# Cross-attention with layer norm: transposes of the identity ahead of x, x evacuated by two engines, and another order of loads, statistics and queries up to slot 2

## The chip, the cores and the metric

The kernel runs on one core of a Trainium2 chip. The metric is the device time of one execution in microseconds (us).

## The reference

Everything is float32. x has 8 batches of 256 rows of 1024; the context has the same shape and serves as keys and as values; there are 32 heads of 32.

```python
xn = (x - mean) * rsqrt(var + 1e-5) * gamma + beta
Q, K, V = split_heads(xn @ Wq.T), split_heads(ctx), split_heads(ctx)
scores = einsum('bhsd,bhtd->bhst', Q, K) * 32 ** -0.5    # masked
attn = einsum('bhst,bhtd->bhsd', softmax(scores), V)      # heads merged again
return x + attn @ Wout.T
```

## The kernel before

**Work and slots.** A unit of work n is one batch and one group of four heads, so there are 64 units, eight to a batch. Slot n of the main loop does the scores of unit n+1, the values of unit n-2, the projection of the batch before, one or two queries that later slots need, and the softmax of unit n+1. The schedule is manual: each engine does its instructions in the order in which the program issues them, and semaphores join the engines. A DMA is issued on SyncE's queue, in program order too.

**A softmax** (`softmax_parts`) takes four tiles, one for each head, each in a PSUM bank of its own (pool `ps_s`, four banks). VectorE adds the mask and finds the row minimum (L391), ScalarE takes the exponential with its sum (L395), VectorE inverts the sum (L402), GpSimd multiplies (L404, `normalize`), VectorE transposes 32x32 blocks (L410, `blocks`), ScalarE copies a part aside (L416), and four DMAs finish the transposition. `new_q` are queries that ScalarE copies out of PSUM after the exponentials; `fill` is a list of other pieces of work that `fill_in` puts between these steps; `between` are loads issued between the four DMAs.

**Queries.** `make_q` (L316) projects eight chunks of normalized x with eight of Wq into one PSUM bank, `copy_q` (L324, L326, L330) takes it to SBUF. The second query of a slot uses the bank of the projection and follows the softmax in program order. `BATCH0` says how many queries each of the first eight slots makes; after that each slot makes one. An fp32 matmul shows as two instructions in the profile, a transpose as one.

**The lead-in.** Only the first batch takes x through TensorE with gamma and beta in the evacuation. `ln_stats` (L205 to L211) takes the statistics of one half of the rows (s = 0 or 1), its last step a power on GpSimd; `ln_norm` (L224 on VectorE) normalizes. `transpose_x0(s)` puts eight 128x128 transposes into two PSUM banks, four in each (L238). `copy_x0` evacuates one of the eight, on ScalarE (L247) or VectorE (L249), with gamma and beta. `first_q(s)` multiplies them with the first part of Wq (L258) and ScalarE copies one half of query 0 (L262). Batch 1 is transposed in slots 0 and 1 (`transpose_x1`, L275, and `copy_x1`, L279 and L281), without gamma: `fold` (L339) multiplies Wq by gamma on GpSimd, one part in each slot. Later batches are transposed by VectorE and DMAs. GpSimd also makes sums of Wout (`sum_wo`, L172) and of the attention output (L522) for a projection with seven products instead of eight (L532; its third product is S2).

Of the kernel before, what the change touches and what calls it, by code (L numbers as in the profile page):

```python
# [46 lines left out]
F32 = mybir.dt.float32  # L47
# [12 lines left out]
def xattn_kernel(  # L60
# [52 lines left out]
    ctx.enter_context(tc.manual_schedule())  # L113


    xs, ks, vs, rs = {}, {}, {}, {}

    def load_x(b, s, h=None):

        if b not in xs:  # L120
            xs[b] = xp.tile([P, NS, D], F32, tag="x", name=f"x_{b}")
        cols = ds(0, D) if h is None else ts(h, 512)
        nc.sync.dma_start(xs[b][:, s, cols], x[b, ts(s, P), cols])
# [31 lines left out]
    def load_wq(o):  # L155
        nc.sync.dma_start(wq[:, o], wq_[o])
# [20 lines left out]
        for h in range(2):  # L177
            load_x(0, s, h)
    load_wq(0)
    for s in range(NS):  # L180
        load_x(1, s)
    load_wq(1)
    load_k(0)
    nc.sync.dma_start(mk, mask.to_broadcast([P, B, T]))
    for o in range(2, 5):
        load_wq(o)
    load_k(2)
    load_v(0)
    load_wq(5)


    xnTs, qs, mvs, rstds = {}, {}, {}, {}
# [3 lines left out]
    def ln_stats(b, s, parts=range(3)):  # L196

        if s == 0 and 0 in parts:
            mvs[b] = sm.tile([P, NS, 2], F32, tag="mv", name=f"mv_{b}", bufs=2)
            rstds[b] = sm.tile([P, NS], F32, tag="rstd", name=f"rstd_{b}", bufs=2)  # L200
        if 0 in parts:
            sts[b, s] = sm.tile([P, 2, 6], F32, tag="st", name=f"st_{b}_{s}", bufs=2)
        for h in range(2):
            if h in parts:
                nc.vector.bn_stats(sts[b, s][:, h, :], xs[b][:, s, ts(h, 512)])  # L205
        if 2 not in parts:
            return
        nc.vector.bn_aggr(mvs[b][:, s, :], sts[b, s].rearrange("p h k -> p (h k)"))
        ve = sm.tile([P, 1], F32, tag="ve", name=f"ve_{b}_{s}", bufs=2)
        nc.vector.tensor_scalar(ve, mvs[b][:, s, 1:2], LN_EPS, None, ALU.add)  # L210
        nc.gpsimd.tensor_tensor(rstds[b][:, s : s + 1], ve, mhalf[:, :1], ALU.pow)  # L211

    def ln_norm(b, s, engine):
        if engine is nc.scalar:
            shift = sm.tile([P, 1], F32, tag="shift", name=f"shift_{b}_{s}", bufs=2)
            nc.gpsimd.tensor_scalar(
                shift, mvs[b][:, s, 0:1], rstds[b][:, s : s + 1], -1.0, ALU.mult, ALU.mult
            )
            engine.activation(
                xs[b][:, s, :], xs[b][:, s, :], AF.Identity,  # L220
                bias=shift, scale=rstds[b][:, s : s + 1],
            )
            return
        engine.tensor_scalar(  # L224
            xs[b][:, s, :], xs[b][:, s, :], mvs[b][:, s, 0:1], rstds[b][:, s : s + 1],
            ALU.subtract, ALU.mult,
        )
# [5 lines left out]
    def transpose_x0(s):  # L233

        for g in range(2):
            px0[s, g] = ps_v.tile([P, NC // 2, P], F32, tag="pv", name=f"px0_{s}_{g}")
            for i in range(NC // 2):
                nc.tensor.transpose(  # L238
                    px0[s, g][:, i, :], xs[0][:, s, ts(NC // 2 * g + i, P)], ident
                )  # L240
# [7 lines left out]
        else:  # L248
            nc.vector.tensor_scalar(to, pt, g, b, ALU.mult, ALU.add)  # L249

    def first_q(s):

        if s == 0:
            pqs[0] = ps_q.tile([P, 512], F32, tag="pq", name="pq_0")
            qs[0] = qp.tile([P, S + 1], F32, tag="q", name="q_0")
        cols = ds(0, P) if s == 0 else ds(P, P + 1)
        for c in range(NC):
            nc.tensor.matmul(  # L258
                pqs[0][:, cols], wq[:, 0, c, :], xnT0[:, c, cols],
                start=(c == 0), stop=(c == NC - 1),  # L260
            )
        nc.scalar.activation(qs[0][:, cols], pqs[0][:, cols], AF.Copy, scale=NEG_SCALE)  # L262

# [82 lines left out]
    def mask_bias(b):  # L346

        mbs[b] = sm.tile([P, T], F32, tag="mb", name=f"mb_{b}", bufs=2)
        nc.vector.tensor_scalar(mbs[b], mk[:, b, :], 1.0, -MASKED, ALU.subtract, ALU.mult)
# [11 lines left out]
                    start=True, stop=True,  # L361
                )

    def softmax(*args):
        for _ in softmax_parts(*args):
            pass

    def softmax_parts(n, new_q=(), between=(), hooks={}, fill=()):

        fill = list(fill)

        def fill_in():
            if fill:
                fill.pop(0)()

        pss = scs[n]
        pT = pTs[n] = ptp.tile([P, 2, NI, NH, NS, K], F32, tag="pT", name=f"pT_{n}")  # L380
        pc = asp.tile([P, NI, NH, NS, K], F32, tag="pc", name=f"pc_{n}")
        es, mns, dens = {}, {}, {}

        def exps(j, part=range(NS)):
            if 0 in part:
                es[j] = ep.tile([P, NS, T], F32, tag="e", name=f"e_{n}_{j}")
                mns[j] = sm.tile([P, NS], F32, tag="mn", name=f"mn_{n}_{j}")
                dens[j] = sm.tile([P, NS], F32, tag="den", name=f"den_{n}_{j}")
            e, mn, den = es[j], mns[j], dens[j]
            for s in part:  # L390
                nc.vector.tensor_tensor_reduce(  # L391
                    out=e[:, s, :], in0=pss[j][:, s, :], in1=mbs[n // NQ], scale=1.0,
                    scalar=NO_SCORE, op0=ALU.add, op1=ALU.min, accum_out=mn[:, s : s + 1],
                )
                nc.scalar.activation(  # L395
                    e[:, s, :], e[:, s, :], AF.Exp, bias=mn[:, s : s + 1], scale=-1.0,
                    accum_out=den[:, s : s + 1],
                )

        def normalize(j):  # L400
            rden = sm.tile([P, NS], F32, tag="rden", name=f"rden_{n}_{j}")
            nc.vector.reciprocal(rden, dens[j])  # L402
            for s in range(NS):
                nc.gpsimd.tensor_scalar(  # L404
                    es[j][:, s, :], es[j][:, s, :], rden[:, s : s + 1], 1.0,
                    ALU.mult, ALU.mult,
                )

        def blocks(j):
            nc.vector.transpose(  # L410
                pT[:, :, :, j, :, :].rearrange("p a i s k -> p (a i) s k"),
                es[j].rearrange("p s (b t) -> p b s t", t=K),
            )

        def aside(j):
            nc.scalar.copy(pc[:, :, ts(j, 2)], pT[:, 1, :, ts(j, 2)])  # L416

        if n == 0:
            for j in range(NH):
                exps(j, (0,))  # L420
            yield
            exps(0, (1,))
            exps(1, (1,))
            exps(2, (1,))
        else:
            exps(0)
            for done in list(pvs):
                copy_at(done)
            exps(1)
            exps(2)  # L430
        normalize(0)
        exps(3, (1,) if n == 0 else range(NS))
        if n <= NQ:
            for q in new_q:
                copy_q(q)
        for hook in hooks.get(0, ()):
            hook()
        normalize(1)
        fill_in()
        blocks(0)  # L440
        for hook in hooks.get(1, ()):
            hook()
        normalize(2)
        fill_in()
        blocks(1)
        aside(0)
        normalize(3)
        fill_in()
        blocks(2)
        fill_in()  # L450
        blocks(3)
        while fill:
            fill_in()
        if n > NQ:
            for q in new_q:
                copy_q(q)
        aside(1)

        for r in range(2):
            nc.sync.dma_start(pT[ts(2 * r, K), 1], pT[ts(2 * r + 1, K), 0])  # L460
        for load in between:
            load()
        for r in range(2):
            nc.sync.dma_start(pT[ts(2 * r + 1, K), 0], pc[ts(2 * r, K)])
        yield

    def values(n):
        pvs[n] = [
# [102 lines left out]


    START = 2
    BATCH0 = (1, 2, 1, 2, 1, 2, 1, 2)
    new_qs, made = [], START
    for n in range(N):
        k = min(BATCH0[n] if n < NQ else 1, N - made)
# [43 lines left out]
    ln_stats(0, 1, (0,))  # L621
    ln_norm(0, 0, nc.vector)
    ln_stats(0, 1, (1, 2))
    nc.gpsimd.tensor_copy(xnT0[:, :, S], bet)
    ln_norm(0, 1, nc.vector)
    ln_stats(1, 0, (0, 1))
    transpose_x0(0)
    for c in range(NC):
        copy_x0(0, c, nc.scalar)
    first_q(0)  # L630
    transpose_x0(1)
    scores(0, (0,))
    for c in range(NC):
        copy_x0(1, c, nc.vector if c % 2 else nc.scalar)
    mask_bias(0)
    first = softmax_parts(
        0, (1,), [partial(load_wq, 6), partial(load_wq, 7)], {},
        [partial(ln_norm, 1, 0, nc.vector), partial(ln_norm, 1, 1, nc.vector)],
    )
    next(first)  # L640
    first_q(1)
    make_q(1, second=True, chunks=range(2))
    scores(0, (1,))
    make_q(1, second=True, chunks=range(2, NC))
    ln_stats(1, 1)
    ln_stats(1, 0, (2,))
    for _ in first:
        pass


    last = None
# [157 lines left out]
```

## Time and profile before

| what | value |
|---|---|
| median of 3 runs | 599.85 us (599.37 to 600.08) |
| profiled execution, its own time | 600.28 us |
| span of the profiled execution | 598.5 us |
| TensorE busy | 579.2 us (97%) |
| VectorE busy | 462.4 us (77%) |
| ScalarE busy | 404.4 us (68%) |
| GpSimd busy | 346.7 us (58%) |
| TensorE busy in 0 to 100 us | 87.87 us |
| TensorE busy in 100 to 500 us | 399.99 us |

PE is TensorE's matmuls, PEld its weight loads, DVE VectorE, ACT ScalarE, POOL GpSimd, SP SyncE; a q after the name is the engine's queue. An L with a number is the line of the kernel. Groups read "line engine operation output<-inputs": px is x transposed in PSUM, xnT the normalized x transposed, pq a query in PSUM, q the query in SBUF, sc the scores, e the exponentials, pT the probabilities transposed. Matmuls are pipelined, so that a busy TensorE need not be one at its peak.

### The profile page before, as it was taken

What the parts mean: (1) busy time and instruction counts of PE and PEld (TensorE: products, weight loads), DVE (VectorE), ACT (ScalarE), POOL (GpSimd) and SP (SyncE); (2) the same over time, 40 slices, a digit from 0 to 9 for tenths busy, and PEclk for the clock granted to TensorE, in tenths of its full rate; (3) what the DMA queues carried; (4) which work ended last, traced back from release to release, by engine and by line L of the source; (5) the groups of instructions that cost most, each with busy time, mean ns of one, the idle gap of its engine ahead of it and who ended that gap; (6) DMA issues with size and microseconds to landing.
All of it is one profiled execution on the core that took longest, in us unless ns stands there. A gap on an engine that the chain in (4) does not pass through costs nothing.

```text
span 598.5 us, 18847 instructions
## 1 busy us (share of the span) xinstructions
PE 579.2 (97%) x6648; PEld 386.7 (65%) x6648; DVE 462.4 (77%) x1677; ACT 404.4 (68%) x1378; POOL 346.7 (58%) x628
## 2 busy tenths in 40 slices
PE   5789999999999999999999999999999999998897
PEld 4578877666766666766666667666676666654443
DVE  4879888788887978788787887878786677779901
ACT  3677788677767767776766876777676576667700
POOL 1468898889448444666438553584545554386600
PEclk9989999999999999999999999999999999999999
DMA  8477678545764557634774556644555364465541
GB/s 310 150 217 222 191 224 245 172 126 155 211 182 143 154 150 222 194 84 155 202 204 144 141 154 171 208 133 132 178 155 168 108 174 141 114 188 176 161 126 70
DMA packets 42063, 101.13 MB, mean 169 GB/s; under 512 B 8560, under 2 KB 8560, under 8 KB 41968
## 3 DMA queue, kind: packets, MB, share of 16 engines
q1 hardware_dynamic: 41680, 99.91, 56.8%
q8 instruction: 53, 0.87, 0.6%
q14 instruction: 42, 0.34, 0.2%
q10 hardware_dynamic: 288, 0.01, 0.0%
HBM read 51.65 MB, written 8.39 MB: 100 GB/s over the span
## 4 chain that ended last, share of the span: by engine, by line
PE 84%; POOL 5%; DVE 5%; ACT 2%; issue 2%; DMA 1%; SPq 0%; POOLq 0%; DVEq 0%
PE pq L316 33%; PE po_S L532 18%; PE pv L475 10%; PE sc L359 10%; PE po_A L532 8%; POOL e L404 5%; PE po L560 3%; DVE e L391 2%; ACT e L395 1%; DVE pT L410 1%; DMA x<-in_x_dram 1%; PE pq L258 1%; PE po_last L560 0%; PE px L238 0%; POOL wq L339 0%
## 5 line engine op out<-in xcount | busy, mean ns | idle before, releaser
L404 POOL TENSOR_SCALAR e<-e,rden 128x256 f32<-128x256 f32 x512 | 237.1, 480 | 175.1 <-DVE rden L402 172.1
L395 ACT ACTIVATE e<-e,mn 128x256 f32<-128x256 f32 x512 | 253.8, 501 | 54.6 <-DVE mn L391 53.4
L316 PE MATMUL pq<-xnT,wq 128*128 128x256 f32 (+1 forms) x1008 | 232.4, 384 | 0.2 <-ACT q L326 0.2
L410 DVE STREAM_TRANSPOSE pT<-e 128x512 f32<-128x512 f32 x256 | 181.3, 709 | 53.8 <-POOL e L404 44.7
L316 PEld LDWEIGHTS pq<-xnT,wq 128*128 128x128 f32 x1008 | 190.1, 191 | 44.3 <-issue 18.0
L391 DVE CUSTOM_DVE_ANT_0 e<-sc,mb 128x256 f32<-128x256 f32 x512 | 185.1, 417 | 32.0 <-PE sc L359 31.3
L416 ACT COPY pc<-pT 128x512 f32<-128x512 f32 x128 | 79.1, 618 | 86.9 <-DVE pT L410 54.7
L532 PE MATMUL po_S<-wo,at 128*128 128x512 f32 x224 | 106.9, 603 | 2.0 <-DVE u L544 1.3
L395 ACT ACTIVATION_READ_ACCUMULATOR e<-e,mn 128x1 f32 x512 | 98.0, 191 | 0.0
L359 PEld LDWEIGHTS sc<-k,q 32*128 32x128 f32 x1024 | 46.4, 184 | 51.0 <-issue 20.9
L359 PE MATMUL sc<-k,q 32*128 32x256 f32 x1024 | 74.1, 401 | 4.9 <-ACT q L324 3.2
L475 PE MATMUL pv<-pT,v 64*32 64x128 f32 x4096 | 74.3, 274 | 0.9 <-ACT at L487 0.9
L475 PEld LDWEIGHTS pv<-pT,v 64*32 64x32 f32 x4096 | 57.1, 105 | 23.5 <-issue 14.4
L532 PEld LDWEIGHTS po_S<-wo,at 128*128 128x128 f32 x224 | 40.7, 189 | 37.1 <-issue 31.8
L532 PE MATMUL po_A<-wo,at 128*128 128x512 f32 x112 | 51.9, 598 | 0.0
L402 DVE RECIPROCAL rden<-den 128x2 f32<-128x2 f32 x256 | 39.3, 154 | 7.5 <-ACT e L395 5.1
L391 DVE DVE_READ_ACCUMULATOR2_ANT mn<- 128x1 f32 x512 | 42.6, 83 | 0.0
L532 PEld LDWEIGHTS po_A<-wo,at 128*128 128x128 f32 x112 | 20.8, 190 | 19.1 <-issue 17.9
L211 POOL TENSOR_TENSOR rstd<-ve,mhalf 128x1 f32<-128x1 f32 x16 | 8.8, 549 | 41.3 <-DVE ve L210 41.3
L487 ACT COPY at<-pv 128x128 f32<-128x128 f32 x128 | 26.0, 251 | 8.2 <-PE pv L475 8.2
L330 ACT ACTIVATE q<-pq,qb 128x256 f32<-128x256 f32 x48 | 22.5, 470 | 9.5 <-PE pq L316 9.5
L532 PE MATMUL po_S<-wo,s 128*128 128x512 f32 x56 | 26.9, 606 | 0.6 <-DVE r L552 0.6
(51 smaller groups left out, 293.8 us busy)
## 6 DMA issues: line engine op xcount, KB each, us to landing
v<-in_kv_dram SPq DMA_DIRECT2D x32, 512.0 KB, 4.6
pT<-pT SPq DMA_DIRECT2D x128, 128.0 KB, 2.3
pT<-pc SPq DMA_DIRECT2D x128, 128.0 KB, 4.1
k<-in_kv_dram SPq DMA_DIRECT2D x32, 256.0 KB, 3.3
x<-in_x_dram SPq DMA_DIRECT2D x14, 512.0 KB, 5.0
r<-in_x_dram SPq DMA_DIRECT2D x28, 256.0 KB, 4.5
out_dram<-r SPq DMA_DIRECT2D x28, 256.0 KB, 3.0
xnT<-xe SPq DMA_DIRECT2D x96, 64.0 KB, 3.3
```

What stands on the lines that cost most here:

```text
L316: nc.tensor.matmul(pqs[n], wq[:, o, c, :], xnTs[b](c), start=(c == 0), stop=(c == NC - 1),)
L330: nc.scalar.activation(q[:, :S].rearrange("p (s a k) -> p a s k", s=NS, a=NA), pqs.pop(n).rearrange("p (a s k) -> p a s k", s=NS, a=NA), A ...
L359: nc.tensor.matmul(scs[n][j][:, s, :], qs[n][r, ts(s, P)], ks[n - n % 2][r, n % 2, :], start=True, stop=True,)
L391: nc.vector.tensor_tensor_reduce(out=e[:, s, :], in0=pss[j][:, s, :], in1=mbs[n // NQ], scale=1.0, scalar=NO_SCORE, op0=ALU.add, op1=ALU.m ...
L395: nc.scalar.activation(e[:, s, :], e[:, s, :], AF.Exp, bias=mn[:, s : s + 1], scale=-1.0, accum_out=den[:, s : s + 1],)
L402: nc.vector.reciprocal(rden, dens[j])
L404: nc.gpsimd.tensor_scalar(es[j][:, s, :], es[j][:, s, :], rden[:, s : s + 1], 1.0, ALU.mult, ALU.mult,)
L410: nc.vector.transpose(pT[:, :, :, j, :, :].rearrange("p a i s k -> p (a i) s k"), es[j].rearrange("p s (b t) -> p b s t", t=K),)
L416: nc.scalar.copy(pc[:, :, ts(j, 2)], pT[:, 1, :, ts(j, 2)])
L475: nc.tensor.matmul(pvs[n][r][j * HD : (j + 1) * HD], vs[n - n % 2][ts(r, 2 * K), i, ds(n % 2 * P + j * HD, HD)], pT[ts(r, 2 * K), :, i, j, ...
L487: nc.scalar.copy(ats[b][:, c, :, ts(r, 2), :], pv.rearrange("p a s k -> p s a k"))
L532: nc.tensor.matmul(pos[b], operand(b, name)[:, c], wo[:, which, c], start=begins and c == 0, stop=c == NK - 1, skip_group_check=not begins,)
```

## The change

Before x arrives, TensorE makes 32 transposes of the identity into a PSUM tile that nothing reads. Eight tiles of the first half of x are evacuated by both engines (six by ScalarE, two by VectorE), those of the second half by bank: the first bank by ScalarE, the second by VectorE. k of the first units and the mask are loaded ahead of x of batch 1, and the last two parts of Wq at the start and not in the first softmax. The first softmax is no longer cut in two: its exponentials follow the copy of both halves of query 0, and the statistics of x of batch 1 become pieces between its steps. Slots 0 to 7 make 2, 2, 1, 1, 2, 1, 2, 1 queries and no longer 1, 2, 1, 2, 1, 2, 1, 2.

```diff
--- before.py
+++ after.py
@@ -113,6 +113,11 @@
     ctx.enter_context(tc.manual_schedule())
 
 
+    busy = ps_s.tile([P, P], F32, tag="sc", name="busy")
+    for _ in range(32):
+        nc.tensor.transpose(busy, ident, ident)
+
+
     xs, ks, vs, rs = {}, {}, {}, {}
 
     def load_x(b, s, h=None):
@@ -177,16 +182,17 @@
         for h in range(2):
             load_x(0, s, h)
     load_wq(0)
-    for s in range(NS):
-        load_x(1, s)
-    load_wq(1)
     load_k(0)
     nc.sync.dma_start(mk, mask.to_broadcast([P, B, T]))
+    load_x(1, 0)
+    load_wq(1)
+    load_x(1, 1)
     for o in range(2, 5):
         load_wq(o)
     load_k(2)
     load_v(0)
-    load_wq(5)
+    for o in range(5, 8):
+        load_wq(o)
 
 
     xnTs, qs, mvs, rstds = {}, {}, {}, {}
@@ -248,16 +254,16 @@
         else:
             nc.vector.tensor_scalar(to, pt, g, b, ALU.mult, ALU.add)
 
-    def first_q(s):
+    def first_q(s, chunks=range(NC)):
 
         if s == 0:
             pqs[0] = ps_q.tile([P, 512], F32, tag="pq", name="pq_0")
             qs[0] = qp.tile([P, S + 1], F32, tag="q", name="q_0")
         cols = ds(0, P) if s == 0 else ds(P, P + 1)
-        for c in range(NC):
+        for c in chunks:
             nc.tensor.matmul(
                 pqs[0][:, cols], wq[:, 0, c, :], xnT0[:, c, cols],
-                start=(c == 0), stop=(c == NC - 1),
+                start=(c == chunks[0]), stop=(c == chunks[-1]),
             )
         nc.scalar.activation(qs[0][:, cols], pqs[0][:, cols], AF.Copy, scale=NEG_SCALE)
 
@@ -361,11 +367,7 @@
                     start=True, stop=True,
                 )
 
-    def softmax(*args):
-        for _ in softmax_parts(*args):
-            pass
-
-    def softmax_parts(n, new_q=(), between=(), hooks={}, fill=()):
+    def softmax(n, new_q=(), between=(), hooks={}, fill=()):
 
 
 
@@ -416,20 +418,20 @@
             nc.scalar.copy(pc[:, :, ts(j, 2)], pT[:, 1, :, ts(j, 2)])
 
         if n == 0:
-            for j in range(NH):
-                exps(j, (0,))
-            yield
-            exps(0, (1,))
-            exps(1, (1,))
-            exps(2, (1,))
+            for s in range(NS):
+                for j in range(NH):
+                    exps(j, (s,))
+            fill_in()
+            normalize(0)
+            fill_in()
         else:
             exps(0)
             for done in list(pvs):
                 copy_at(done)
             exps(1)
             exps(2)
-        normalize(0)
-        exps(3, (1,) if n == 0 else range(NS))
+            normalize(0)
+            exps(3)
         if n <= NQ:
             for q in new_q:
                 copy_q(q)
@@ -462,7 +464,6 @@
             load()
         for r in range(2):
             nc.sync.dma_start(pT[ts(2 * r + 1, K), 0], pc[ts(2 * r, K)])
-        yield
 
     def values(n):
         pvs[n] = [
@@ -571,7 +572,7 @@
 
 
     START = 2
-    BATCH0 = (1, 2, 1, 2, 1, 2, 1, 2)
+    BATCH0 = (2, 2, 1, 1, 2, 1, 2, 1)
     new_qs, made = [], START
     for n in range(N):
         k = min(BATCH0[n] if n < NQ else 1, N - made)
@@ -621,31 +622,28 @@
     ln_stats(0, 1, (0,))
     ln_norm(0, 0, nc.vector)
     ln_stats(0, 1, (1, 2))
+    transpose_x0(0)
+    early, late = (0, 1, 2, 3, 6, 7), (4, 5)
+    for c in early + late:
+        copy_x0(0, c, nc.vector if c > 5 else nc.scalar)
     nc.gpsimd.tensor_copy(xnT0[:, :, S], bet)
     ln_norm(0, 1, nc.vector)
+    first_q(0, early + late)
     ln_stats(1, 0, (0, 1))
-    transpose_x0(0)
-    for c in range(NC):
-        copy_x0(0, c, nc.scalar)
-    first_q(0)
+    mask_bias(0)
     transpose_x0(1)
     scores(0, (0,))
     for c in range(NC):
-        copy_x0(1, c, nc.vector if c % 2 else nc.scalar)
-    mask_bias(0)
-    first = softmax_parts(
-        0, (1,), [partial(load_wq, 6), partial(load_wq, 7)], {},
-        [partial(ln_norm, 1, 0, nc.vector), partial(ln_norm, 1, 1, nc.vector)],
-    )
-    next(first)
+        copy_x0(1, c, nc.scalar if c < NC // 2 else nc.vector)
     first_q(1)
     make_q(1, second=True, chunks=range(2))
     scores(0, (1,))
     make_q(1, second=True, chunks=range(2, NC))
-    ln_stats(1, 1)
-    ln_stats(1, 0, (2,))
-    for _ in first:
-        pass
+    softmax(0, (1,), (), {}, [
+        partial(ln_stats, 1, 1, (0,)), partial(ln_stats, 1, 1, (1, 2)),
+        partial(ln_stats, 1, 0, (2,)),
+        partial(ln_norm, 1, 0, nc.vector), partial(ln_norm, 1, 1, nc.vector),
+    ])
 
 
     last = None
```

## The prediction

> **What bounds the kernel now.** I read the waits of TensorE first, then the windows, then the order of time.
>
> The waits of TensorE over the whole run (what waited, for whom: us in total, times, longest):
>
> ```profile
> PE px L238 <- DVE x L224: 7.0, 1, 7.0
> PE sc L359 <- ACT q L324: 3.2, 2, 2.7
> PE sc L359 <- ACT q L262: 1.7, 1, 1.7
> PE pq L316 <- ACT q L326: 0.2, 1, 0.2
> ```
>
> All but the last lie in the first 32 us, and TensorE is busy in 100 of the 100 us of each of four later windows (100 to 500). So the run is a lead-in of some 43 us with holes, then a stretch that TensorE fills. The change edits the lead-in; its gain is how much earlier the full stretch begins, if the other engines begin it earlier too.
>
> The windows (stretch, its length, busy us of PE, PEld, DVE, ACT, POOL, then the granted clock, DMA share, GB/s):
>
> ```profile
> 7.02:8.78 1.76, 1.76 (x8) 1.67 (x9) 1.02 (x4) 0.60 (x2) 0.70 (x2) 1.00 1.04 421
> 8.78:12.19 3.41, 3.41 (x17) 3.41 (x17) 1.89 (x3) 2.29 (x7) 0.00 (x1) 1.00 1.04 368
> 12.19:15.60 3.41, 3.41 (x30) 2.67 (x28) 1.18 (x4) 2.00 (x5) 0.00 (x0) 1.00 1.01 376
> 29.26:32.67 3.41, 1.15 (x17) 0.80 (x17) 2.90 (x9) 3.19 (x11) 3.24 (x9) 1.00 0.92 267
> 32.68:36.08 3.40, 3.40 (x8) 2.73 (x9) 3.39 (x17) 2.65 (x10) 2.42 (x4) 0.50 0.65 205
> ```
>
> The clock column has no record before 12.19 and prints 1.00; the pace tells: eight transposes fill 7.02 to 8.78, 0.22 us each, and 17 instructions fill 8.78 to 12.19, but at 12.23 transposes go at 0.11. TensorE begins at half speed. It falls back once, at 32.68, after a stretch of 3.41 us in which it worked 1.15: eight instructions in 3.40 us where sixteen would fit, 1.7 us lost.
>
> The order of time (start, us, engine, what; in brackets the idle time before and who ended it):
>
> ```profile
> 7.02 1.97 PE L238 MATMUL px<-ident,x 128*128 128x128 f32 x8 [7.02 <-DVE x L224]
> 8.18 2.90 ACT L247 ACTIVATE xnT<-px,bet,gam 128x128 f32<-128x128 f32 x8 [2.34 <-PE px L238]
> 12.23 1.04 PE L238 MATMUL px<-ident,x 128*128 128x128 f32 x8
> 13.36 0.41 DVE L249 TENSOR_SCALAR xnT<-px,gam,bet 128x128 f32<-128x128 f32 x1 [2.69 <-ACT xnT L247]
> 13.81 0.81 ACT L247 ACTIVATE xnT<-px,bet,gam 128x128 f32<-128x128 f32 x2 [0.48 <-DVE xnT L249]
> 14.30 0.76 DVE L249 TENSOR_SCALAR xnT<-px,gam,bet 128x128 f32<-128x128 f32 x2 [0.53 <-ACT xnT L247]
> ...
> 18.80 0.25 ACT L262 ACTIVATE q<-pq 128x129 f32<-128x129 f32 x1
> 19.10 0.71 PE L359 MATMUL sc<-k,q 32*128 32x256 f32 x8 [1.69 <-ACT q L262]
> ```
>
> The two evacuating engines take turns (13.36, 13.81, 14.30): 3.1 us for eight tiles. The copy of the first query's second half (18.80) stands behind four exponentials on ScalarE, and the scores wait for it.
>
> VectorE later, by the same columns, and what it waits for:
>
> ```profile
> 38.49 0.69 DVE L281 COPY xnT<-px 128x512 f32<-128x512 f32 x1 [2.22 <-PE px L275]
> ...
> 43.47 0.42 DVE L391 CUSTOM_DVE_ANT_0 e<-sc,mb 128x256 f32<-128x256 f32 x1 [0.94 <-PE sc L359]
> ...
> 98.83 0.42 DVE L391 CUSTOM_DVE_ANT_0 e<-sc,mb 128x256 f32<-128x256 f32 x1 [0.28 <-PE sc L359]
> ```
>
> From 43.47 to 98.83 VectorE waits for TensorE nowhere: VectorE and GpSimd set the pace of slots 3 to 9, and TensorE hides them by 0.2 us (its wait on L326). The lead-in pays only as far as the softmax chain comes earlier.
>
> **What the Trainium skill says.** TensorE: Matmul & The Clock Gate, Part 1: the clock is halved by default and released after a busy window of about 3.4 us, windows running freely. The trace agrees: half-speed stretches of 3.4 us, changes of the clock a whole number of them apart (12.19, 32.68, 36.09). Its Part 4 says that transposes do not count as busy for this gate in the same way. The trace leaves that open: the full window before the release at 12.19 held matmuls only. PSUM — Partial Sum Buffer, section on bank collisions: two engines on one bank must be kept apart, on two banks they need not. The trace agrees: within a bank they take turns (above), while L247 for tile 4 (second bank) ran from 14.17 beside L249 at 14.30.
>
> **The change part by part**, by clock times as in the trace; the gain at a point is before minus after.
>
> *Warm-up.* 32 transposes start when the identity stands (its last instruction ends at 1.29). At 0.213 us all would last to 8.2; if the release comes at W, the rest go at 0.109. A window that lies wholly after 1.3 ends between 4.8 and 8.2, so they end between 6.5 and 8.2; x is ready at 7.02 as before. Delay 0 to 1.2, I take 0.3 and start from 7.02.
>
> *First half of x.* Warm, four transposes are out at 7.6. ScalarE copies six tiles at 0.362 (2.90/8) instead of eight, to 9.85; VectorE does the other two beside it from 8.1 (0.76). They stand ahead of the second normalization: that ends at 9.7 instead of 9.5, still ahead of its transposes. The first query ends at 10.1 instead of 12.2.
>
> *Loads.* SyncE issues k and the mask before x of batch 1, none added; wq 6 and 7 leave the softmax's queue for the start. x of batch 1 then follows 2.0 MB and ends at 2.5 MB; by the windows 46 GB/s for 2.5 us, 342 for 5, 419 for 2.2 are 2.7 MB at 9.7, when VectorE asks for it. Cost nothing; if late, VectorE's mask and copies queue behind it.
>
> *Second half of x.* Transposes 10.2 to 11.1, scores 11.2 to 11.9, ScalarE's four tiles 10.8 to 12.3 beside VectorE's four 11.3 to 12.7, so eight take 1.9 instead of 3.1. The sixteen matmuls (0.112 each) now bound: 11.9 to 13.7 (before 16.5). Its copy comes before the exponentials: ready 14.25 (19.05). Two chunks of query 1, then scores: VectorE starts on the second half at 15.25 instead of 19.84, gain **4.6**.
>
> *Softmax 0.* Part is given back. The statistics of x 1 (two of 0.65, small ones 0.8) and all eight exponentials (0.49) now follow; ScalarE ends them at 18.2. GpSimd has eight multiplications (4.65) with two powers (0.55) between them, and VectorE's first normalization of x 1 waits for the second power (20.5), blocking two transposes queued behind it, which TensorE doesn't need yet. Last transpose 24.1 instead of 26.6: gain **2.5**.
>
> *Queries (2,2,1,1,...).* Slot 0 has query 3 as well: 3.5 us of matmuls that fill TensorE's hole of 2.7. Scores 1 at 18.7, query 2 to 23.25, x 1's transposes 24.1, query 3 27.6; scores 2 wait for ScalarE's copy of query 2, 31.47 less 2.5, so 29.0. The hole is 1.4, less than the 2.3 of 3.41 that cost the clock; no half-speed window. Query 4 to 33.6, transposes 34.5, query 5 38.0, scores 3 to 39.2 (before 43.47): gain **4.3**. Here VectorE has waited 0.5 and 0.9 instead of 2.2 and 0.9. The added copies of queries 3 and 5 (0.37) fall where ScalarE's matmuls are done long before.
>
> *Slots 3 to 10.* VectorE and GpSimd keep their pace from there, 4.3 ahead, and use up their waits of 0.28 (98.83) and about 0.4: the GpSimd sum that the S2 product needs ends at 112.22, the product started at 112.64. TensorE by itself would be 6.5 ahead, so it waits about 2 us in slot 5 (one query instead of two), and again at S2. Gain 4.3+0.3+0.4 = **5.0**, less the 0.3 of the warm-up: **4.7**. The query counts sum to 12 by slot 7 in both, so nothing behind is moved.
>
> The profiled execution took 600.28 (span 598.5, 1.8 around it); 600.28-4.7 = 595.6; the median lies 0.43 below it: **595.2**.
>
> **Rivals.**
> (1) *Warm-up transposes don't release the clock.* For: Part 4 above; against: the trace has no case. The 32 then end at 8.2, x's start 1.2 late and slow, the first query ends at 13.4, and the sixteen matmuls of its second half at 16.9 or 17.7 instead of 13.7: 3.2 to 4.0 lost of 5.0. Gain 1.0 to 1.8: 598.0 to 598.9.
> (2) *Slower: half-clock windows at the new short holes.* Rival 1, and besides TensorE falls back between 14 and 38 us, at the holes before scores 1 (0.8) and scores 2 (1.4), which then stand beside slow work. Each such window costs 1.7 in the part where TensorE leads VectorE to slot 3. One cancels rival 1's gain, two make it slower: 599.85-1.5+3.4 = 601.8. Against it: the only fall so far needed two thirds of a window idle.
> (3) *TensorE alone counts*, VectorE and GpSimd having more slack than two waits show: 6.5-0.3, so 593.6.
>
> **How the numbers follow.** Likeliest case 50% (594.2 to 596.2 by the warm-up's delay and half a microsecond in the handovers), rival 1 35%, rival 2 10%, rival 3 5%. 0.2% is 1.2 us, about what a measurement of this kernel tells from no change: faster is below 598.65. Rival 1 gives 0.23 to faster and 0.12 to same; rival 2 0.01 to same and 0.09 to slower. Faster 0.78, same 0.13, slower 0.09. The range from 593.5 to 599.4 leaves out most of rival 2 and the ends.
>
> **What would show it.** Right: eight transposes of x in about 1.0 us instead of 1.97; L249 beside L247; no clock of 0.50 at 30 to 40; scores 3 near 39; a wait of 2 us on TensorE near 65. Wrong: transposes of x at 0.21 us (rival 1), a 0.50 window in 14 to 38 (rival 2), S2 starting over 6 us earlier (rival 3), or VectorE waiting for x of batch 1.

## The result and the profile after

The changed kernel takes **598.86 us** (median of 16 runs, 598.52 to 599.21); the kernel before, beside it, 599.93 (598.93 to 600.91). The ratio is 0.9983, with a 95% interval of 0.9975 to 0.9991: some 1.0 us, or 0.17%, where 4.7 had been forecast. The profiled execution took 598.86 (span 597.1) against 600.28 (598.5), so the two traces show 1.4 of gain.

The waits of TensorE in the changed kernel, as before (what waited, for whom: us in total, times, longest):

```profile
PE sc L365 <- ACT q L330: 3.5, 2, 2.0
...
PE busy L118 <- POOL ident masks.py:199: 1.3, 1, 1.3
...
PE pq L264 <- ACT xnT L253: 0.4, 1, 0.4
PE sc L365 <- DVE mn L393: 0.2, 1, 0.2
```

The wait of 7.0 us for x is gone, for the 32 transposes fill it; the waits of scores for a copied query have shrunk from 4.9 us in three (L262 and L324) to 3.5 in two (L330). The waits of the lead-ins come to 11.9 and 5.2 us: TensorE has lost 6.7 us of waits, and the kernel 1. (The last line is a wait in slot 6. Three more waits, 3.5 us behind 150 us, which the prediction's list leaves out, stand in both kernels.)

The windows of the changed kernel (length, busy us of PE, PEld, DVE, ACT, POOL, granted clock, DMA share, GB/s):

```profile
1.34:6.55 5.21, 5.21 (x25) 5.21 (x26) 2.68 (x6) 1.28 (x1) 0.56 (x1) 1.00 0.88 255
6.56:9.97 3.41, 2.96 (x26) 2.76 (x25) 2.97 (x7) 1.92 (x6) 0.71 (x2) 1.00 1.00 341
...
71.42:74.81 3.39, 3.26 (x53) 2.48 (x37) 2.96 (x6) 2.25 (x7) 3.28 (x8) 0.50 0.91 283
```

25 instructions fill the first 5.21 us, 0.21 each: half speed, which the clock column has no record of. From 6.56 on they go at 0.11. TensorE had done nothing else before, so transposes alone do release the clock. The half-clock window that stood at 32.68 has gone, and another stands at 71.41, in slot 6.

The lead-in in order of time:

```profile
1.34 6.24 PE L118 MATMUL busy<-ident 128*128 128x128 f32 x32 [1.34 <-POOL ident masks.py:199]
...
7.42 1.04 PE L244 MATMUL px<-ident,x 128*128 128x128 f32 x8
...
11.32 1.29 DVE L211 BATCH_NORM_STATS2 st<-x 128x6 f32<-128x512 f32 x2 [1.37 <-DMA x<-in_x_dram]
...
11.79 0.71 PE L365 MATMUL sc<-k,q 32*128 32x256 f32 x8
...
12.71 1.37 DVE L255 TENSOR_SCALAR xnT<-px,gam,bet 128x128 f32<-128x128 f32 x4
...
15.42 0.71 PE L365 MATMUL sc<-k,q 32*128 32x256 f32 x8
...
16.15 0.42 DVE L393 CUSTOM_DVE_ANT_0 e<-sc,mb 128x256 f32<-128x256 f32 x1 [2.08 <-PE sc L365]
...
26.60 0.39 DVE L393 CUSTOM_DVE_ANT_0 e<-sc,mb 128x256 f32<-128x256 f32 x1
```

VectorE at the same places in the kernel before, where the second half of the scores began at 19.10:

```profile
16.35 0.42 DVE L391 CUSTOM_DVE_ANT_0 e<-sc,mb 128x256 f32<-128x256 f32 x1
...
26.52 0.39 DVE L391 CUSTOM_DVE_ANT_0 e<-sc,mb 128x256 f32<-128x256 f32 x1
```

Two lines of the changed kernel matter. At 16.15 VectorE makes the first reduction of the *first* half of the scores. That half began at 11.79 and VectorE was free from 14.08; it waits 2.08 us for TensorE all the same, until the *second* half (15.42) is out. In the kernel before it reduced the first half (16.35) ahead of the second (19.10). And at 26.60 softmax 1 begins, where it began at 26.52 in the kernel before: all that TensorE and the evacuations had won by then is spent.

### The profile page after: what moved, and what is told of

Read it like the earlier page. It is cut to its first block, busy times and chain, and to the rows that moved or that the text cites. A ratio compares the mean times of both kernels' runs of the same rounds, so it can differ in the third digit from the quotient of the medians.

```text
span 597.1 us, 18913 instructions
## 1 busy us (share of the span) xinstructions
PE 584.1 (98%) x6680; PEld 390.4 (65%) x6680; DVE 463.0 (78%) x1679; ACT 402.9 (67%) x1376; POOL 346.6 (58%) x628
## 4 chain that ended last, share of the span: by engine, by line
PE 79%; POOL 9%; DVE 7%; issue 2%; ACT 1%; POOLq 0%; DVEq 0%
PE pq L322 31%; PE po_S L533 17%; PE sc L365 9%; PE pv L476 9%; PE po_A L533 7%; POOL e L406 6%; PE po L561 3%; DVE e L393 3%; DVE pT L412 1%; PE busy L118 1%; POOL wo L177 1%; ACT e L397 1%; PE pq L264 1%; POOL at L523 1%; DVE st L211 0%
## 5 line engine op out<-in xcount | busy, mean ns | idle before, releaser
L365 PE MATMUL sc<-k,q 32*128 32x256 f32 x1024 | 75.7, 401 | 3.8 <-ACT q L330 3.5
L533 PEld LDWEIGHTS po_A<-wo,at 128*128 128x128 f32 x112 | 20.8, 190 | 19.1 <-issue 18.2
```

Source lines behind the costliest of these rows:

```text
L365: nc.tensor.matmul(scs[n][j][:, s, :], qs[n][r, ts(s, P)], ks[n - n % 2][r, n % 2, :], start=True, stop=True,)
L533: nc.tensor.matmul(pos[b], operand(b, name)[:, c], wo[:, which, c], start=begins and c == 0, stop=c == NK - 1, skip_group_check=not begins,)
```

## The experiments

Their question: where the forecast's 4.7 us went. Each kernel was run beside the kernel before; ratios are against that, and times of different experiments are best compared by their ratios.

**Reductions ahead of the second scores.** Both halves of one head's scores lie in one PSUM bank. In the changed kernel the program issues the second half's scores before the first half's reductions; in the kernel before it was the other way round.

The line added in the lead-in (the definition of `reduce_first`, which makes VectorE's four reductions of the first half, and their removal from the softmax are left out here):

```diff
+    reduce_first()
     scores(0, (1,))
```

> The changed kernel with one thing moved: VectorE's four reductions of the first half of the first scores are issued before TensorE's scores of the second half, which go into the same four banks (the exponentials stay where they are). Theory (program order on a shared bank): in the changed kernel these reductions start at 16.15, when the second half of the scores is out, though the first half is out at 12.5; here they start at about 14.1, after VectorE's evacuations, exponentials at 14.9 instead of 16.6, softmax 1 begins at 24.9 instead of 26.6, and the time falls by 1.0 to 1.7 us against the changed kernel, to about 597.5. Rival (the softmax chain of slots 3 to 9 sets its own pace and swallows the lead): softmax 1 begins earlier as well, but the time stays within 0.4 us of the changed kernel's.

Measured: ratio 0.9972 (0.9961 to 0.9983), median 598.13: 0.7 us below the changed kernel by the ratios, of 1.0 to 1.7 expected. VectorE:

```profile
14.18 0.42 DVE L371 CUSTOM_DVE_ANT_0 e<-sc,mb 128x256 f32<-128x256 f32 x1
...
16.34 0.42 DVE L371 CUSTOM_DVE_ANT_0 e<-sc,mb 128x256 f32<-128x256 f32 x1 [0.70 <-PE sc L365]
...
25.42 0.38 DVE L371 CUSTOM_DVE_ANT_0 e<-sc,mb 128x256 f32<-128x256 f32 x1
```

The first reduction starts at 14.18 and softmax 1 at 25.42 instead of 26.60. The runs lie from 597.35 to 600.03, and their mean granted clock sorts them. One half-clock window of 3.41 us is 0.003 of the mean. Nine runs with none or one of them took 597.35 to 598.45, four with two (mean 0.994) took 599.29 to 600.03. The profile is one of these four; its windows:

```profile
69.13:75.94 6.81, 6.81 (x83) 4.96 (x76) 6.24 (x22) 5.25 (x20) 6.15 (x11) 0.50 0.65 203
```

So the order on the bank was about half of the loss in softmax 0 (1.2 us here of the 2.3 by which softmax 1 missed the forecast), and a second thing takes the gain away in slot 6.

**The two ways round: counts alone, all but the counts.** `BATCH0` of the changed kernel in the kernel before, and of the kernel before in the changed one.

```diff
-    BATCH0 = (1, 2, 1, 2, 1, 2, 1, 2)
+    BATCH0 = (2, 2, 1, 1, 2, 1, 2, 1)   # counts alone; the other run undoes this line
```

> The kernel before with the query counts 2,2,1,1,2,1,2,1 alone. Theory (all that the change gained comes from query 3 in slot 0, which fills TensorE's hole and saves the half-clock window): TensorE has no half-clock window at 32 us, scores 3 start at 40.7 instead of 42.3, and the gain is the whole gain of the change, 1.0 to 1.4 us, so about 598.7. Rival (the lead-in gave it): the time is that of the kernel before within 0.4 us.

Measured: 1.0002 (0.9993 to 1.0011), median 600.15. The half-clock window at 32 is gone and scores 3 start at 40.70, both as expected, but the time is that of the kernel before: the theory that the counts made the whole gain fell. A half-clock window stands at 71.55 in this trace too, but it is not the reason: the nine runs without one (mean clock 1.0) took 599.08 to 600.91, their median is 600.14.

> The changed kernel with the query counts of before, 1,2,1,2,1,2,1,2. Theory (the lead-in's gain is lost to the late reductions): softmax 1 begins at 26.6 as before and the time is that of the kernel before within 0.4 us, with TensorE's hole ahead of scores 2 back. Rival (the lead-in gave the gain): about 598.9.

Measured: 1.0017 (1.0008 to 1.0026), median 601.43: neither, it is slower. With TensorE ahead and no query 3 to make, its wait ahead of scores 2 grows from 2.7 to 4.9 us, and two half-clock windows follow (all 16 runs have the mean clock of two, 0.994):

```profile
31.03:37.84 6.81, 5.91 (x25) 4.38 (x26) 5.33 (x24) 5.42 (x20) 5.35 (x11) 0.50 0.46 108
```

**Without the warm-up.** The changed kernel without the 32 transposes:

```diff
-    for _ in range(32):
-        nc.tensor.transpose(busy, ident, ident)
```

> The changed kernel without the 32 transposes of the identity. Theory (they release the clock, and the chain through the second scores depends on it): transposes of x at 0.21 us and the first query at 0.21 an instruction, its second half ends at about 15.7 instead of 14.5, the first reductions start at 17.4 instead of 16.15, and the time rises by 1.0 to 1.4 us, to about 600. Rival (the lead-in isn't on the path at all): the time stays within 0.4 us of the changed kernel's.

Measured: 1.0004 (0.9994 to 1.0013), median 600.54: by the ratios the warm-up is worth 1.3 us, as expected. The profiled execution, 599.61, is the quickest of its 14 runs (599.61 to 601.36), and the trace shows less of it:

```profile
6.87 1.97 PE L241 MATMUL px<-ident,x 128*128 128x128 f32 x8 [6.87 <-DVE x L227]
```

x is transposed at half speed again, but the clock was released at 10.39 already, and softmax 1 begins at 26.95, only 0.35 later than in the changed kernel. The changed kernel's 16 runs spread over 0.7 us.

**Keeping the clock in slot 6.** TensorE in the changed kernel:

```profile
67.63 2.07 PE L365 MATMUL sc<-k,q 32*128 32x256 f32 x6
69.89 1.13 PE L365 MATMUL sc<-k,q 32*128 32x256 f32 x10 [0.19 <-DVE mn L393]
...
80.81 1.15 PE L365 MATMUL sc<-k,q 32*128 32x256 f32 x16
```

The sixteen matmuls of scores 7, which follow one another within 1.15 us elsewhere, spread over 3.4 (67.63 to 71.02): they wait, head by head, for VectorE to reduce scores 6 in the same banks. The profile counts most of this wait of some 2 us as busy. The edit puts sixteen transposes of the identity into it, in the free bank of `ps_o` (the loop that makes them, `keep_clock`, is left out here):

```diff
+    KEEP = {6: 16}
...
+        if n in KEEP:
+            keep_clock(n, KEEP[n])
         if n + 1 < N:
             scores(n + 1)
```

> The changed kernel with 16 transposes of the identity on TensorE at the start of slot 6, where it waits some 2 us for the reductions that free the score banks (they go into the free query bank). Theory (this new wait costs the clock, and the half-clock window comes when slot 6 has two queries to make, so TensorE falls behind the softmax chain again): no window at 0.50 near 70, scores 8 start near 79.1 instead of 80.8, and the time falls by 0.3 to 0.9 us against the changed kernel, to about 598.2. Rival (TensorE has slack there, as the prediction said): the time stays within 0.2 us of the changed kernel's.

Measured: 0.9984 (0.9978 to 0.9991) against 0.9983 for the changed kernel: the rival held. The window at 71 is gone, and TensorE's order of time says where its lead goes:

```profile
67.92 1.97 PE L654 MATMUL keep<-ident 128*128 128x128 f32 x16 [0.43 <-ACT q L332]
...
79.70 1.15 PE L365 MATMUL sc<-k,q 32*128 32x256 f32 x16
...
110.97 2.84 PE L533 MATMUL po_S<-wo,at 128*128 128x512 f32 x6 [1.08 <-POOL at L523]
```

Scores 8 start at 79.70 instead of 80.81, 1.1 earlier; then TensorE waits 1.08 at the S2 product for GpSimd's sum, and starts it at 110.97 where the changed kernel started at 111.05. One half-clock window in slot 6 is paid out of TensorE's slack. The runs of the changed kernel itself say so too: 598.79 to 599.21 for the five without such a window (mean clock 1.0), 598.52 to 599.13 for the eleven with one or two.

The same with the reductions ahead as well, the two diffs together:

> The changed kernel with both edits: the first four reductions ahead of the scores of the second half, and the 16 transposes in slot 6. Theory: the runs of the reductions alone spread over 2.7 us, 597.4 to 598.5 with the clock at 1.0 and 599.3 to 600.0 with two half-clock windows; here none has them, so the median is about 597.4 and the spread under 1 us. Rival (the spread comes from the lead-in's clock, not from slot 6): median and spread stay at 598.1 and 2.7 us.

Measured: 0.9953 (0.9941 to 0.9966), median 597.45, five runs from 597.24 to 597.64. VectorE's order of time with both edits:

```profile
13.64 0.42 DVE L371 CUSTOM_DVE_ANT_0 e<-sc,mb 128x256 f32<-128x256 f32 x1
...
15.81 0.42 DVE L371 CUSTOM_DVE_ANT_0 e<-sc,mb 128x256 f32<-128x256 f32 x1 [0.70 <-PE sc L365]
...
24.88 0.39 DVE L371 CUSTOM_DVE_ANT_0 e<-sc,mb 128x256 f32<-128x256 f32 x1
```

The first half is reduced before TensorE writes the second into the banks (scores from 15.08); the second follows at 15.81 and softmax 1 begins at 24.88, 1.7 us before that of the changed kernel (1.4, if both are counted from the start of the first scores, 11.46 and 11.79). No run has a half-clock window in slot 6 any more, where four of 13 had two, but five runs are few. And the median is some 0.8 below that of the nine runs without two windows (598.08), each against the kernel before beside it: what else the 16 transposes gain here stays open.

**Statistics behind the reductions.** VectorE's `ln_stats(1, 0, (0, 1))` moved behind the reductions, added to both edits:

```diff
-    ln_stats(1, 0, (0, 1))
     mask_bias(0)
...
     reduce_first()
+    ln_stats(1, 0, (0, 1))
     scores(0, (1,))
```

> As the run with both edits, and VectorE's statistics of the first half of x of batch 1 moved behind the first reductions. Theory (the moved loads made x of batch 1 late: VectorE waits for it until 11.3 to 11.5, and the mask and four evacuations stand behind that wait): evacuations start near 11.5 instead of 12.9, the first reductions at 12.9 instead of 14.2, softmax 1 begins 0.4 to 0.8 us earlier, and the time falls by as much, to about 596.8. Rival (TensorE's sixteen matmuls and the exponentials set the pace by then): no change beyond 0.2 us.

Measured: 0.9950 (0.9938 to 0.9962), median 597.24, 0.2 below the run before it, with intervals that overlap. The first scores start at 11.87 and 11.46 in the two profiles; counted from them the first reductions begin at 1.39 and 2.18, but softmax 1 at 13.31 and 13.42. VectorE's wait for x of batch 1 is real, but next to nothing of it reaches softmax 1.

**Counts and kept clock** in the kernel before (the line of counts above, and `keep_clock` in slot 6):

> The kernel before with the new query counts and the 16 transposes in slot 6. Theory (the counts gain 1.6 us by slot 3 and lose it to the half-clock window in slot 6): 1.0 to 1.6 us faster than the kernel before, about 598.6. Rival (the gain of slot 3 is lost elsewhere): as with the counts alone, the time of the kernel before within 0.4 us.

Measured: 0.9988 (0.9980 to 0.9995), median 599.19, half of what was expected; its softmax 3 begins 1.8 earlier than before (41.65), its softmax 11 1.4 (106.15). With the counts alone the runs without a half-clock window were no faster than the kernel before, so sparing that window does not account for the 0.8 us that the 16 transposes gain by the ratios; their cause stays open.

**The copy of query 9.** Slot 4 makes two queries in the changed kernel, and in the kernel before slots 3 and 5 do. The second query's copy is issued behind the softmax of its slot, so that it stands ahead of the next softmax's exponentials on ScalarE. GpSimd in the changed kernel:

```profile
69.35 0.93 POOL L406 TENSOR_SCALAR e<-e,rden 128x256 f32<-128x256 f32 x2
70.50 2.90 POOL L406 TENSOR_SCALAR e<-e,rden 128x256 f32<-128x256 f32 x6 [0.22 <-DVE rden L404]
```

After two multiplications it waits for an inverted sum that ScalarE's exponentials hold up.

The edit, on the changed kernel with `reduce_first()`:

```diff
-    BATCH0 = (2, 2, 1, 1, 2, 1, 2, 1)
+    BATCH0 = (2, 2, 1, 2, 1, 2, 1, 1)
```

> The changed kernel with the first reductions ahead (as in that run), no transposes in slot 6, and the query counts 2,2,1,2,1,2,1,1, so that slots 3 and 5 make two queries and not slots 4 and 6. Theory (two things are paid in slots 4 to 6: TensorE's wait of 2 us, and the copy of query 9 on ScalarE, which stands ahead of the exponentials of softmax 6 and holds GpSimd up by 0.36): neither is there, softmax 7 begins 7.5 us after softmax 6 and not 7.9, no half-clock window near 70, and the median is 597.1 with a spread under 1 us, 0.3 less than with the transposes. Rival (one of the two remains): 597.45 as with the transposes, or a spread of 2 us as with the reductions alone.

Measured: 0.9949 (0.9936 to 0.9961), median **596.98**, five runs from 596.74 to 597.10. GpSimd at the same place:

```profile
68.00 3.71 POOL L421 TENSOR_SCALAR e<-e,rden 128x256 f32<-128x256 f32 x8
```

Eight multiplications without a break; softmax 7 begins 7.54 after softmax 6 (73.02 and 65.48), where the changed kernel needed 7.88, and 7.89 with the 16 transposes. So the copy was the cause there, not the clock. This version has the lowest median, though its interval overlaps those of the two versions with the reductions ahead and transposes in slot 6; it needs no such transposes, for TensorE makes one query more in slot 5 instead.

**The warm-up alone, and with counts and kept clock**, in the kernel before. The first run adds this, the second also the counts and `keep_clock`:

```diff
+    busy = ps_s.tile([P, P], F32, tag="sc", name="busy")
+    for _ in range(32):
+        nc.tensor.transpose(busy, ident, ident)
```

> The kernel before with the 32 transposes of the identity alone. Theory (they release the clock before x, and in the kernel before the reductions of the first half come ahead of the second scores, so that their gain is not lost): first query 2 us earlier, softmax 1 begins at about 24.6 instead of 26.5, scores 3 2 us earlier, the hole and the half-clock window near 30 stay; about 598.0, more than the whole change gains. Rival (lost at the hole, whose length then costs a second window): 599.5 to 601.

Measured: 0.9989 (0.9980 to 0.9997), median 599.33, between the two and nearer to the rival. Softmax 1 begins at 26.01, not 24.6. The clock sorts these runs too: 597.28 to 597.37 for the three without a half-clock window, 597.98 to 600.00 for 16 with one, 600.70 and 601.02 for two with two.

> The kernel before with the 32 transposes of the identity, the new query counts and the 16 transposes in slot 6: the change without its evacuations side by side, its loads and its order of statistics. Theory (what remains of these is small once the clock is up): softmax 1 begins at about 24.6, softmax 3 at 40.4, and the time is 597.5, as with both edits on the changed kernel. Rival (the evacuations and the earlier copy of the query are worth what the prediction said): 598.5 or more, since softmax 1 begins a microsecond or more later than there (24.88).

Measured: 0.9980 (0.9972 to 0.9988), median 598.69; softmax 1 begins at 25.24, softmax 3 at 41.18. The rival's time held, though not its reason: softmax 1 comes 0.4 later than with both edits (24.88), and softmax 3 1.0 (40.14). TensorE:

```profile
8.45 2.65 PE L262 MATMUL pq<-xnT,wq 128*128 128x128 f32 x16 [0.40 <-DMA wq<-in_wq_dram]
...
12.85 0.71 PE L363 MATMUL sc<-k,q 32*128 32x256 f32 x8 [0.88 <-DMA k<-in_kv_dram]
...
17.80 0.50 PE L363 MATMUL sc<-k,q 32*128 32x256 f32 x4 [1.39 <-ACT q L266]
...
30.91 1.15 PE L363 MATMUL sc<-k,q 32*128 32x256 f32 x16
```

With the clock up, the scores wait 0.88 for k, which this kernel loads behind x of batch 1, and 1.39 for the copy behind the exponentials. It stays late by this: it reaches scores 2 at 30.91 without a wait, where with both edits they started at 29.88 after a wait of 1.56. So this kernel lacks the moved loads and the earlier copy; that they, and not the evacuations side by side, make the whole difference was not tried.

## Why the prediction was wrong

The direction held, and 598.86 lies in the range; the size did not. It is the time that rival 1 named, but by coincidence, for its cause is not there: the transposes release the clock. Of the 3.4 us between the forecast 4.7 and the 1.3 by which the last softmax came earlier in the traces, 2.3 are missing at softmax 1, 0.1 between softmax 1 and 3, and 1.0 behind softmax 3.

- *Warm-up:* right. The release came at 6.56, x's transposes began at 7.42, 0.4 late (0.3 taken), eight of them in 1.04 us. Only the bounds for the release, 4.8 to 8.2, were too narrow: in other traces with these transposes it came as early as 4.08.
- *First half of x:* right. The two engines work side by side (L253 from 8.05, L255 from 8.49), and the first query ends at about 10.8, where the sum has 10.1+0.3.
- *Loads, "cost nothing":* wrong. x of batch 1 came at 11.3, not by 9.7. The estimate took the rate of the kernel before, 2.7 MB by 9.7; the changed kernel's trace has 247 GB/s up to there, 2.4 MB. It also took the transfers to land one after the other in the order of issue; by that, x would have come at 10.0 (252 GB/s, 2.5 MB). Why the rate is lower and the order does not hold wasn't tried. The price was small (the run with the statistics behind).
- *Second half of x, "VectorE starts on the second half at 15.25 instead of 19.84":* **the step that failed.** It took the first half's reductions for done by then. They were issued behind the second scores, which write into the same banks, and waited for them: they began at 16.15 instead of 12.7, the exponentials at 16.62 instead of 14.25, and these ended at 20.6 instead of 18.2. The gain at softmax 1, 2.5-0.3, was -0.1; with the four reductions moved, softmax 1 began at 25.42, 25.23 and 24.88 in three traces instead of 26.60, so that 1.2 to 1.7 came back. The Trainium skill's page PSUM — Partial Sum Buffer, section on bank collisions, which the prediction cites for ScalarE beside VectorE, says the same of a TensorE write and a reader; the trace's 2.08 us agrees, and the prediction had not applied it there. (Here the two halves are one tile as well as one bank; which of the two makes VectorE wait, no run separates.)
- *Queries:* right. Softmax 1 to softmax 3 took 15.26 us, 15.1 by its sum (39.2-24.1), and the window at 30 to 40 is gone: gain 1.6 at softmax 3, none of it left from softmax 0.
- *Slots 3 to 10, "+0.3+0.4":* wrong in sign. It counted two waits as usable and looked at the copies of second queries only for what they wait for. The copy of query 9 cost 0.34 (the run with counts 2,2,1,2), and using up the wait at 98.83 did not help, since softmax 11 was not reached through it (GpSimd's multiplications of softmax 10 began at 100.41 for 101.63, 1.2 earlier): gain 1.6 at softmax 3 and at softmax 10, 1.2 at softmax 11, 1.3 at the last.
- *"It waits about 2 us in slot 5":* right (it shows at the start of slot 6), but the prediction did not ask what it does to the clock. The half-clock windows of rival 2 came there, at 71 and not between 14 and 38. In the changed kernel slack pays for one; in the kernel with the reductions moved the runs with two took 1.4 us more (medians 599.47 and 598.08).

The trace of the kernel before was itself a late case. Its lead-in stands unchanged in two more traces, with the counts alone and with counts and kept clock: their clock was released at 10.11 and 9.86 instead of 12.20, and softmax 1 began at 25.93 and 25.71 instead of 26.52. So softmax 1 moves by 0.8 us between executions of one lead-in, most likely with the release of the clock, and the -0.1 can as well be -0.9.

What is not split up: with the reductions moved, softmax 1 is still 0.5 to 1.0 later than the 24.1+0.3 of the sum, and the runs alone do not say which of the later x, the second query's matmuls and the exponentials make that up.

## What to carry to other kernels

Two halves of a tile in one PSUM bank were one thing for the order of engines here: issue the reader of the first half before the writes of the second, or it waits for both. Where a change puts an engine ahead, look for the place where it then stands still, and for what stillness costs there: for TensorE a wait of some 2 us was followed by a half-clock window here, and 16 transposes in that wait kept it away. And before a copy is called free, ask what is queued behind it, not only what it waits for.

## What the hardware showed

- Transposes of the identity alone, 0.213 us each, released TensorE's clock 5.2 us after the first. The Trainium skill's TensorE: Matmul & The Clock Gate, Part 4, says that transposes do not count in the same way; for these fp32 transposes the measurement decides.
- Nine traces begin with these 32 transposes, all at 1.34 or 1.35, and the release comes at 4.08 to 7.29: where the windows of the clock fall differs from one execution to the next. In the earliest case TensorE had worked for 2.74 of the last 3.41 us. In the latest it had worked for 2.53 of the 3.41 us that ended one window before the release, at 3.88, and that released nothing. By these two, if windows follow one another every 3.41 us, an estimate is that a window counts as busy from somewhere between three quarters and four fifths of it.
- The runs of one program spread by it where their mean clock sorts them: 3.7 us with the warm-up alone, 2.7 where two windows may come in slot 6. The spread is 1.75 us for the changed kernel without the warm-up, 0.7 with it, and 0.4 in the versions at 597.45 and 596.98, in five runs each; that the first release makes the 1.75 is likely, but their mean clock does not show it.
